# A third state's dt*u*B by TensorE in the even sequences from the fifth on, in a kernel of a selective scan and a mixture of experts

## The chip, the cores and the metric

The kernel runs on one core of one Trainium2 chip. The metric is the time of one execution on the device, in microseconds (us). One execution was profiled by the hardware; all durations, waits and windows come from it.

The core's engines work side by side, each through its own queue of instructions: PE multiplies matrices (TensorE; its weight loads are shown as PEld), DVE is VectorE, ACT is ScalarE, POOL is GpSimd, and SP is SyncE, which issues most of the DMAs.

## The reference, cut to what matters

The input is 16 sequences of 512 positions with 256 features. The first layer is a selective scan in both directions, the second a soft mixture of 16 experts; after each the input is added and normalized. The part that the change concerns is the scan. For each of 512 channels d and 16 states n:

```
dA = einsum('bld,dn->bldn', dt, A)
dB_u = einsum('bld,bld,bln->bldn', dt, u, B)
dA_cum = exp(the sum of dA over the later positions)
xs = cumsum(dB_u * dA_cum, 1) / (dA_cum + 1e-12)
y = einsum('bldn,bln->bld', xs, C) + u * D
```

So for each state, dt*u (a value for each channel and position) is multiplied by B of that state (one value for each position, the same for all channels). Then a recurrence runs along the positions, its result is gated (from the 1e-12) and multiplied by C, and all states are summed.

## The kernel before

**The scan.** A sequence b has four parts, `scan_part(b, r, p, ...)`: direction r (0 forward, 1 backward) and half p of the channels. A part has two chunks of 128 channels and runs over the 16 states in pairs (n and n + 1), so it has 8 x 2 = 16 steps; a sequence has 64 steps and the kernel 1024. A step has positions along the free axis (512) and channels on the 128 partitions. It does:

1. POOL: `db` = dt*u times B of both states, L442, B having been spread over the partitions by a DMA (`bs`, L431).
2. ACT: the decay exp(dt*A) of each state, L459, and a tanh, L461, for the gate.
3. DVE: the recurrence of each state (L465 forward, L467 backward) and the gate (L470), into `hg`.
4. POOL: `hg` times C of both states, L471 (`cs`, L432).
5. PE: transposes of `hg`, summed in PSUM over all states and both directions, L386. This is emitted two steps later (`add_up(2)`, L485), and `hg` has four buffers.

**States by TensorE.** For the states that `diag_of(b)` names (L280), step 1 is done by PE: L420 multiplies the transposed dt*u (`duT`) by a matrix that has B of the state on its diagonal (`dg`), four matmuls of 128 positions each. The result lies in a PSUM bank, and DVE's recurrence reads it there. These states are always the second of a pair. POOL's L442 is then half as wide (k = 1), the `bs` load half as large, and the decay of that state goes to SBUF (`dec`) instead of a PSUM bank of the ring `h` (three banks).

The diagonals are made in DRAM: `project_unit` writes B of the chosen states at the diagonal places of zeroed blocks with one DMA from ACT's queue (L306), once for each sequence and direction. A `dg` load (L435, 256 KB, one buffer) is issued by SP one pair of states ahead (`n + 3 in ds`). Sequences 0 to 2 have four such states (3, 7, 11, 15), all later ones two (5, 13).

**Work beside the scan.** Everything else is written as generators in three lists, `prep` (the next part's projections), `front` (the end of the sequence before: output projection, normalization, dispatch to the experts' slots) and `back` (experts and their combination, for two sequences at a time). After each scan step `beside_scan` (L556) takes at most one piece of each. A piece takes one or two PSUM banks of a pool of three (`mps`, by `bank`, L107) and holds them until the next step consumes them (`yield HOLD`). `piece` (L519) takes a piece only where the oldest bank still held, and all taken since, leave room in the three. A product of L420 takes its bank from the same pool: `by_diagonal` (L414) is called in the step before the one that uses it (L478), and L483 ends its claim.

`front` and `back` are paced: each step adds to a credit the share of the steps left (at most 2.0 is kept), and a piece costs 1. `back` gets experts(g) and combine(2g), combine(2g+1) at each odd sequence from the fourth on, spread over the 128 steps of that sequence and the following even one. So an odd sequence from the sixth on holds mostly expert work and an even one mostly combination: in each chunk of 128 positions logits `cl` (L933), their exponential, transposes `ctp` (L954), and the product `cpo` (L1015). What `front` has not done at a sequence's end is emitted at once (`front.drain()`); what `back` has not done stays in its list. After the last scan, whatever is left runs with eight banks.

The emission fixes the program order. `late(...)` marks instructions that are kept in it.

Of the kernel before, what the change touches and what calls it, by code (L numbers as in the profile page):

```python
# [55 lines left out]
def seq_layers(tc, ident, neghalf, a, out):  # L56
# [22 lines left out]
    with ExitStack() as ctx:  # L79
# [199 lines left out]

        def diag_of(b):  # L280

            return (3, 7, 11, 15) if b < 3 else (5, 13)

        def project_unit(b, r, out):

            w = side[r]
            q = f"{b}_{r}"
            yield GAP + 1
            px = bank(f"px_{q}")
            for c in range(ND):  # L290
                nc.tensor.matmul(
                    px[:XW, :], w["xT"][:, c, :], out["u"][:, c, :], start=(c == 0), stop=(c == ND - 1)
                )
            yield HOLD
            xd = p1.tile([XW, L], F32, tag=f"xd_{r}", name=f"xd_{q}")
            bc = dram.tile([2, NS, L], F32, tag="bc", name=f"bc_{q}")
            if r == 0:
                late(nc.scalar.activation(xd, px[:XW, :], AF.Identity, bias=unit))
            else:

                late(nc.scalar.activation(xd[: XB + NS, :], px[: XB + NS, :], AF.Identity, bias=unit[: XB + NS]))
                nc.scalar.copy(xd[XC:XW, :], px[XC:XW, ::-1])
            nc.sync.dma_start(bc[0], xd[XB : XB + NS, :])
            nc.sync.dma_start(bc[1], xd[XC:XW, :])
            ds = diag_of(b)
            nc.scalar.dma_start(  # L306
                diag_dram[r, : len(ds)].rearrange("i l (p s) -> i l p s", p=P)[:, :, :, 0],
                xd[XB + ds[0] : XB + NS : ds[1] - ds[0], :].rearrange("i (l p) -> i l p", p=P),
            )
            out.update(xd=xd, bc=bc)  # L310
# [96 lines left out]
        def scan_part(b, r, p, v, accs, done, then):  # L407

            prep.drain()
            prep.gens += [[1, g] for g in [turn_pair(b, r, p, v)] + then]  # L410
            w, ds = side[r], diag_of(b)
            made = {}

# [733 lines left out]
```

## Time and profile before

| | us |
|---|---|
| median of 3 runs | 5327.67 (5324.82 to 5328.87) |
| the profiled execution | 5322.25 |
| its span, first to last instruction | 5320.5 |
| busy: POOL | 4681.6 (88%) |
| busy: DVE | 4560.6 (86%) |
| busy: PE (matmul) | 4310.4 (81%) |
| busy: ACT | 4104.9 (77%) |
| sequences 4, 6, 8, 10, 12, 14 | 307.9 to 308.7 each |
| sequences 5, 7, 9, 11, 13 | 326.2 to 327.1 each |
| after the last scan | 240.4 |

A sequence is counted from the first L471 of its first step to the first L471 of the next sequence. A line of the profile gives the line of the kernel, engine, operation, what is written and read, the shapes and the count; behind the bar are the busy time and the mean duration in ns; then the idle time of the engine before them and what ended most of it. "Granted clock" is the share of PE's full clock that the throttle let through. A busy PE is not a PE at its peak, since matmuls are pipelined.

### The profile page before, as it was taken

How to read it: one execution, taken by the hardware profiler on the slowest of the kernel's cores; microseconds unless marked ns; L12 is line 12 of the kernel's file. 1: busy time of each engine (PE TensorE's matmuls, PEld its weight loads, DVE VectorE, ACT ScalarE, POOL GpSimd, SP SyncE). 2: the span in 40 equal slices, each digit the busy share in tenths (PEclk: the TensorE clock that was granted, in tenths of full speed). 3: DMA queues.
4: the chain of work that ended last, by engine and by line, in shares of the span. 5: the costliest groups of instructions: out<-in, count | busy, mean ns of one | idle time of the engine just before them, and what ended most of it. 6: DMA issues, size and time to landing. Idle time of an engine off the chain costs nothing. (4 is left out here: it accounts for less than half of the span.)

```text
span 5320.5 us, 74550 instructions
## 1 busy us (share of the span) xinstructions
PE 4310.4 (81%) x24498; PEld 3411.1 (64%) x24498; DVE 4560.6 (86%) x6284; ACT 4104.9 (77%) x6573; POOL 4681.6 (88%) x2537
## 2 busy tenths in 40 slices
PE   5677776897778978788788878889787897878889
PEld 3556565676567756676666766667666676657667
DVE  7999999889998899888898888988898889987733
ACT  6777878887888877888887887888778887777644
POOL 6999999989999899999999989998999989988710
PEclk7778888998899989999899988899888998889999
DMA  5444444675446644576446754467544664447545
GB/s 141 137 129 152 126 142 131 211 234 152 146 146 224 222 144 143 171 226 206 132 140 198 236 169 151 134 210 230 157 151 144 217 227 149 144 153 230 168 135 168
DMA packets 614820, 907.82 MB, mean 171 GB/s; under 512 B 84606, under 2 KB 404734, under 8 KB 614432
## 3 DMA queue, kind: packets, MB, share of 16 engines
q1 hardware_dynamic: 532740, 859.35, 50.9%
q10 hardware_dynamic: 81692, 43.70, 3.1%
q8 instruction: 195, 3.19, 0.2%
q14 instruction: 193, 1.58, 0.1%
HBM read 840.34 MB, written 62.56 MB: 170 GB/s over the span
## 5 line engine op out<-in xcount | busy, mean ns | idle before, releaser
L471 POOL TENSOR_TENSOR hg<-hg,cs 128x1024 f32<-128x1024 f32 x1024 | 2416.9, 2364 | 125.0 <-DVE hg L470 108.0
L442 POOL TENSOR_TENSOR db<-du,bs 128x1024 f32<-128x1024 f32 (+1 forms) x1024 | 2087.7, 2042 | 227.8 <-DVE h L465 84.1
L470 DVE SCALAR_TENSOR_TENSOR hg<-th,h 128x512 f32<-128x512 f32 x1744 | 1156.8, 679 | 183.4 <-PE acc L386 105.9
L386 PE MATMUL acc<-ident,hg 128*128 128x128 f32 x8192 | 1163.6, 292 | 106.4 <-POOL hg L471 84.6
L386 PEld LDWEIGHTS acc<-ident,hg 128*128 128x128 f32 x8192 | 1034.4, 152 | 284.6 <-POOL hg L471 131.3
L467 DVE TENSOR_TENSOR_SCAN h<-h,db 128x512 f32<-128x512 f32 x872 | 1044.9, 1219 | 104.9 <-ACT h L459 92.6
L465 DVE TENSOR_TENSOR_SCAN h<-h,db 128x512 f32<-128x512 f32 x872 | 1044.1, 1219 | 44.5 <-ACT h L459 43.6
L461 ACT ACTIVATE th<-rr,Ah_f 128x512 f32<-128x512 f32 x1024 | 724.6, 714 | 200.9 <-DVE hg L470 198.1
L461 ACT ACTIVATE th<-rr,Ah_b 128x512 f32<-128x512 f32 x1024 | 721.3, 712 | 153.5 <-DVE hg L470 143.5
L459 ACT ACTIVATE h<-dt,A_f 128x512 f32<-128x512 f32 x872 | 591.4, 680 | 99.5 <-DVE hg L470 96.3
L459 ACT ACTIVATE h<-dt,A_b 128x512 f32<-128x512 f32 x872 | 592.3, 680 | 85.6 <-DVE hg L470 81.7
L420 PE MATMUL hd<-dg,duT 128*128 128x128 f32 x2432 | 375.7, 305 | 73.2 <-ACT duT L364 27.1
L420 PEld LDWEIGHTS hd<-dg,duT 128*128 128x128 f32 x2432 | 347.9, 220 | 84.5 <-ACT duT L364 29.5
L710 PE MATMUL pl<-x2T,seT 128*128 128x512 f32 x512 | 294.1, 704 | 78.4 <-DVE hg L470 37.4
L838 PE MATMUL peo<-Wd,ht 128*128 128x256 f32 x1024 | 258.1, 408 | 63.2 <-DVE rr L346 36.6
L869 PEld LDWEIGHTS pg<-st,Wg 128*128 128x128 f32 x2048 | 243.1, 195 | 94.1 <-issue 82.8
L811 PE MATMUL pu<-st,Wu 128*128 128x128 f32 x2048 | 255.6, 284 | 49.3 <-DMA Wu<-in_Wu_dram 27.0
L1015 PE MATMUL cpo<-ceo,ct 128*128 128x256 f32 x1024 | 256.0, 407 | 43.2 <-DVE rr L346 40.0
L811 PEld LDWEIGHTS pu<-st,Wu 128*128 128x128 f32 x2048 | 245.9, 199 | 60.6 <-DVE h L467 29.5
L838 PEld LDWEIGHTS peo<-Wd,ht 128*128 128x128 f32 x1024 | 205.5, 206 | 106.1 <-DVE rr L346 39.2
L869 PE MATMUL pg<-st,Wg 128*128 128x128 f32 x2048 | 265.0, 284 | 4.5 <-DMA st<-s_dram 3.4
L1015 PEld LDWEIGHTS cpo<-ceo,ct 128*128 128x128 f32 x1024 | 207.2, 207 | 87.2 <-DVE rr L346 42.7
(165 smaller groups left out, 6754.0 us busy)
## 6 DMA issues: line engine op xcount, KB each, us to landing
cs<-bc SPq DMA_DIRECT2D x512, 512.0 KB, 3.9
bs<-bc SPq DMA_DIRECT2D x360, 512.0 KB, 5.2
Wg<-in_Wg_dram SPq DMA_DIRECT2D x128, 512.0 KB, 5.7
Wu<-in_Wu_dram SPq DMA_DIRECT2D x128, 512.0 KB, 5.8
Wd<-in_Wd_dram SPq DMA_DIRECT2D x128, 512.0 KB, 5.5
dg<-diag_dram SPq DMA_DIRECT2D x152, 256.0 KB, 4.3
bs<-bc SPq DMA_DIRECT2D x152, 256.0 KB, 3.5
x<-in_x_dram SPq DMA_DIRECT2D x32, 512.0 KB, 6.5
```

What stands on the lines that cost most here:

```text
L386: ins = nc.tensor.matmul(accs[c][:, s], hc[:, j, s], ident, is_transpose=True, start=False, stop=(last and j == 1 and lc == NL - 1),)
L420: ins = nc.tensor.matmul(h[:, s], v[c][3][:, s], dg[:, s], start=True, stop=True)
L442: nc.gpsimd.tensor_tensor(db[:, :k, :], du.unsqueeze(1).to_broadcast([P, k, L]), bs[:, :k, :], ALU.mult)
L459: nc.scalar.activation(hs[j][1], dt, AF.Exp, scale=w["A"][:, c, s])
L461: nc.scalar.activation(ths[j], rr, AF.Tanh, bias=LN_1E12 / 2, scale=w["Ah"][:, c, s])
L465: nc.vector.tensor_tensor_scan(h, dec, add, 0.0, ALU.mult, ALU.add)
L467: nc.vector.tensor_tensor_scan(h[:, ::-1], dec[:, ::-1], add[:, ::-1], 0.0, ALU.mult, ALU.add)
L470: nc.vector.scalar_tensor_tensor(hg[:, j, :], th, 1.0, h, ALU.add, ALU.mult)
L471: nc.gpsimd.tensor_tensor(hg, hg, cs, ALU.mult)
L811: nc.tensor.matmul(pu[:, fc * P : (fc + 1) * P], got["Wu", e][:, k, fc * P : (fc + 1) * P], st[:, k, :, j * SL : (j + 1) * SL], start=(k = ...
L838: nc.tensor.matmul(po[:, j * DM : (j + 1) * DM], ht[:, fc, :], got["Wd", e0 + j][:, fc, :], start=(fc == 0), stop=(fc == NF - 1),)
L869: nc.tensor.matmul(pg[:, fc * P : (fc + 1) * P], got["Wg", e][:, k, fc * P : (fc + 1) * P], st[:, k, :, j * SL : (j + 1) * SL], start=(not ...
```

## The change

One line of `diag_of`:

```
         def diag_of(b):

-            return (3, 7, 11, 15) if b < 3 else (5, 13)
+            return (3, 7, 11, 15) if b < 3 else (5, 13) if b % 2 else (5, 9, 13)
```

Sequences 4, 6, 8, 10, 12 and 14 (counted from 0) now have three states by TensorE: 5, 9 and 13. State 9 is the second of the pair n = 8. In each of the 24 parts of these sequences the two steps of n = 8 have a half-wide L442 and a half-sized `bs` load, there is one `dg` load more (at n = 6) and 8 matmuls of L420 more, and two more steps in which a product holds a bank. `project_unit` writes three rows of diagonals instead of two. Sequence 3 and the later odd ones, and 0 to 2, are as before.

## The prediction

> **What bounds the kernel now.** I read the page first, for the busy shares.
>
> ```profile
> PE 4310.4 (81%) x24498; PEld 3411.1 (64%) x24498; DVE 4560.6 (86%) x6284; ACT 4104.9 (77%) x6573; POOL 4681.6 (88%) x2537
> ```
>
> No engine is full over the span, so the stages must be told apart. A scan step ends in one product of L471 on POOL, and there are 64 steps in a sequence; the start of every 64th gives the borders of the sequences. In the windows view at these borders the columns are the stretch, its length, then busy us of PE, PEld, DVE, ACT and POOL, then the granted clock, the DMA share and GB/s. The rows are sequences 1, 3, 8 (even, touched), 9 (odd, untouched), 15, and what follows the last scan:
>
> ```profile
> 335.90:619.20 283.30, 206.80 (x1172) 168.49 (x1171) 261.16 (x323) 226.14 (x361) 275.68 (x153) 0.82 0.44 137
> 904.80:1226.30 321.50, 277.99 (x1714) 224.86 (x1715) 279.25 (x389) 257.43 (x389) 293.53 (x153) 0.94 0.66 210
> 2496.00:2804.50 308.50, 245.97 (x1282) 186.43 (x1281) 282.68 (x384) 248.87 (x417) 294.99 (x157) 0.88 0.44 140
> 2804.50:3131.50 327.00, 283.58 (x1740) 230.66 (x1738) 284.16 (x398) 261.53 (x398) 295.30 (x157) 0.94 0.67 214
> 4709.70:5080.10 370.40, 311.64 (x1830) 249.92 (x1828) 282.97 (x414) 264.99 (x416) 285.72 (x151) 0.92 0.59 186
> 5080.10:5320.50 240.40, 216.77 (x1216) 177.29 (x1214) 71.71 (x199) 97.36 (x210) 14.68 (x44) 0.97 0.52 160
> ```
>
> The reader is to see that in sequence 8 POOL has 13.5 us of idle time in 308.5 (96% busy) and PE has 62.5. In sequence 9 POOL does the same 295 us, but the sequence is 18.5 us longer, while PE has 37.6 us more work. After the last scan PE is busy for 90% of the time. Sequences 4, 6, 10, 12 and 14 lie at 307.9 to 308.7 us with the rows of 8; the odd ones from 5 to 13 at 326.2 to 327.1. The waits view (total us, times, longest) of DVE in sequence 8 and then in sequence 9 names the difference:
>
> ```profile
> DVE hg L470 <- PE acc L386: 0.8, 1, 0.8
> ```
>
> ```profile
> DVE hg L470 <- PE acc L386: 12.8, 11, 2.4
> ```
>
> In the even sequence nobody waits long for PE. In the odd one DVE's gated state waits for PE to free a buffer of `hg`, and POOL then waits for DVE. So POOL sets the pace of the sequences that the change touches, and PE helps to set it in their neighbours and after the scans.
>
> **What the change removes and adds.** The rows by form (count, then busy us, mean ns):
>
> ```profile
> L442 POOL TENSOR_TENSOR db<-du,bs 128x1024 f32<-128x1024 f32 x720 | 1699.9, 2366 | 181.2 <-issue 70.2 <-DVE h L465 56.5 <-DVE h L467 42.0
> L442 POOL TENSOR_TENSOR db<-du,bs 128x512 f32<-128x512 f32 x304 | 387.9, 1277 | 46.7 <-DVE h L465 27.5 <-POOL hg L471 11.2 <-DMA bs<-bc 4.2
> L420 PE MATMUL hd<-dg,duT 128*128 128x128 f32 x2432 | 375.7, 305 | 73.2 <-ACT duT L364 27.1 <-ACT yt L645 13.6 <-DMA dg<-diag_dram 10.2
> L933 PE MATMUL cl<-seT,cx 128*128 128x512 f32 x480 | 230.2, 620 | 32.6 <-DVE res L277 12.4 <-ACT et L725 10.7 <-DVE hg L470 7.5
> L1015 PE MATMUL cpo<-ceo,ct 128*128 128x256 f32 x1024 | 256.0, 407 | 43.2 <-DVE rr L346 40.0 <-ACT ct L963 2.5 <-DMA ceo<-e_dram 0.4
> ```
>
> Six sequences (4, 6, ..., 14) have four parts each with two chunks: 48 steps of n = 8 change.
>
> Off POOL: 48 products shrink from 2366 to 1277 ns, 1.089 us each: 8.7 us a sequence, 52.3 in all. This is the most that can be won.
>
> On PE: 48 x 4 matmuls of 305 ns = 58.6 us, 9.8 a sequence, against 62.5 of idle time: nothing. Without that cover, by the slope of odd against even (18.5 us for 37.6 of PE, 0.49), it would be 4.8 a sequence.
>
> ACT writes 48 decays to SBUF instead of PSUM (712 against 680 ns): 1.6 us in all, beside 60 us of idle time a sequence: nothing. DVE's scan (1217 against 1219 ns) and its gating (679 both) do not change. A step of n = 8 takes one `h` bank instead of two, which can only help.
>
> DMA: 24 `bs` loads halve and 24 `dg` loads of the same 256 KB come in; bytes stay. SyncE issues 24 more, 0.385 us each, and each waits for the one `dg` buffer, which is free once state 5's second chunk is multiplied, two steps earlier; `bs` and `cs` of n = 8 queue behind it, and have three buffers. In the trace 152 such loads cost PE 10.2 us of waiting in 10 places, so I expect 1 to 2 us of PE waiting: nothing. ACT's write of the diagonals takes three rows for two, two states' time before its first use: nothing.
>
> **What the 8.7 us become.** Part 1 of sequence 8 has POOL at 75.6 of 76.7 us, so there the whole 2.18 us of a part can be won; in part 0 POOL (72.6 of 78.0) is already level with DVE (72.8), so little. DVE does 282.7 us in the sequence; the smallest idle time of DVE in a sequence with other work beside the scan is 22.1 (sequence 1). DVE plus this gives 304.8, a gain of 3.7; the full POOL gain is 8.7. I take 6.5, a little over the middle, because work of DVE leaves these sequences too (next point): **39 us won**, between 22 and 52.
>
> **What the change moves.** This is no instruction of its own. A product of L420 sits in one of three `mps` banks from the step before its use, and while one sits there, `piece` (line 525) lets other work take a bank only if the oldest holder and all after it fit in three. I counted pieces by that rule on paper. In sequence 4 as it is, the three steps around each of states 5 and 13 take 3 or 4 banks of other work, and the steps around state 9 take 6 or 7, because they are free. Closing these too pushes out about 13 banks a sequence; most find room in other steps, because a piece that is refused keeps its credit up to 2. Following the queues through the four parts, I end with one more piece of dispatch to be drained at the end of sequence 4 (`pd` beside `pq`), and with 5 pieces of combine left to the next sequence instead of 1. In the later even sequences about 1 to 3 more would be left, since a longer queue comes in from the odd one. My count can be off by two or three pieces either way.
>
> The prices. A chunk of combine costs PE 8 x 0.48 + 1.25 + 4.0 = 9.1 us (L933: 230.2/60 chunks; L954: 80.0/64; L1015: 256.0/64) in three pieces: 3 us a piece.
> - Drain: 6 ends. Part 0 of the odd sequence is 2.3 us longer than its part 1 now, with one piece drained. 0 to 2.3, I take 1: 6 us.
> - Odd sequences 5 to 13: 1.7 to 3 more pieces each, some 7.5 us of PE. It may fit PE's 43 us of idle time (0) or cost by the slope above (0.49). I take half of it: 1.9 each, 9 us, between 0 and 22.
> - Sequence 15 already runs pieces at every step that lets them, so what it inherits comes out after the scans, where PE is 90% busy: 4 pieces net, 12 us of PE, I take 10, between 0 and 21.
>
> The sum: 39 won, 25 paid: 14 less than the profiled execution's 5322.25 us (span 5320.5 and 1.75 around it), 5308. The median of the runs is 5.4 above that execution, so **5314 us**, 0.26% less.
>
> A rule weighed. By matmul rows PE is 80% busy in even sequences and 87% in odd ones; by weight loads 60% and 71%. The Trainium skill, "Perfetto Trace Analysis", section "Identifying the Most-Contended Engine", says that matmul busy time is a bad measure of PE's headroom and that weight loads' busy share is a good one. By it PE is no limit in the odd sequences, the moved pieces cost nothing there, and the sum would be 9 us lower. The wait of 12.8 us on PE in sequence 9 speaks against that, so the rows keep their price.
>
> **The rivals.**
> - *All of it arrives.* The refused pieces find room within the even sequences, DVE doesn't bind: 40 to 50 us won, little paid, about 5285. For it: POOL is the only full engine there, and sequences 0 to 2 have four diagonal states with POOL at 97 to 99%. Against: these have no expert or combine work beside them. Chance 0.10.
> - *It cancels.* DVE takes POOL's place at once (22 to 25 us won), and the moved pieces eat that: about 5327. For it: POOL and DVE would be within 4 us of each other in the even sequences. Chance 0.22.
> - *Slower.* PE in the odd sequences and after the scans pays for the work pushed out: 3 pieces at 0.49 are 4.4 us in five sequences (22), 7 pieces at the end 21, drains of two pieces 12, together 55 against 30 won: 25 more, about 5350. It decides from some 5 or 6 pieces carried out of each even sequence. For it: 5 is what I count, and sequence 5 is already 4.9 us longer than 3 with 5.9 us more of PE. Against: part of that stretch is PE's idle time. Chance 0.34.
> - That the edit is not in effect: both callers of `diag_of` pass the same b, so I give it nothing.
>
> **How the numbers follow.** My forecast (5314, from 5300 to 5321) has 0.34, the largest with *slower*; I keep it since POOL's gain is priced from rows and the losses rest on a count. A difference under 0.2% (10.7 us) can't be told from no change. Faster by more has 0.34 + 0.10 = 0.44, within 0.22, slower by more 0.34. The range for 8 in 10 takes the full arrival at its low end and the slower case up to its centre: 5285 to 5350.
>
> **What would show it.** The narrow form of L442 should stand at 352, and L420 at 2624. Even sequences should last 301 to 303 us with POOL under 96%; over 306 says that DVE or PE took over. Odd ones should last about 329; at 331 and more the slower rival holds, at 327 the first one. After the last scan 250 us are expected for 240.4. Combine's products (L1015) should be found moving from even into odd sequences; if they stay, my count is wrong.

## The result, and the profile after

The changed kernel takes **5453.93 us** (median of 4 runs, 5441.44 to 5455.07) against 5327.72 for the kernel before: a ratio of **1.0232, 95% interval 1.0215 to 1.025**. It is 126 us slower. I had forecast 5314, with a range up to 5350: the sign and the range were both wrong. The profiled execution's span is 5453.0 us, 132.5 more than before's.

The page's busy shares, in the columns of the line shown first for the kernel before:

```profile
PE 4379.0 (80%) x24882; PEld 3455.5 (63%) x24882; DVE 4557.8 (84%) x6284; ACT 4102.4 (75%) x6572; POOL 4635.0 (85%) x2537
```

POOL does 46.6 us less and PE 68.6 more, as the edit says, and every share falls. So the time is not work: every engine has more idle time. The windows view of the kernel after (stretch, length, busy us of PE, PEld, DVE, ACT, POOL, granted clock, DMA share, GB/s), for the same sequences as before (1, 3, 8, 9, 15, then what follows the last scan):

```profile
335.20:619.70 284.50, 205.26 (x1181) 166.77 (x1180) 262.05 (x324) 227.12 (x363) 276.17 (x154) 0.85 0.44 137
906.00:1228.50 322.50, 279.03 (x1715) 226.20 (x1716) 279.73 (x389) 258.13 (x389) 293.65 (x153) 0.94 0.66 209
2538.70:2859.10 320.40, 251.41 (x1360) 191.32 (x1360) 279.07 (x380) 247.45 (x407) 286.85 (x157) 0.91 0.46 142
2859.10:3190.60 331.50, 281.81 (x1720) 226.99 (x1720) 287.18 (x402) 263.17 (x410) 295.74 (x158) 0.95 0.63 204
4827.30:5204.00 376.70, 313.52 (x1823) 251.64 (x1824) 280.83 (x408) 253.27 (x404) 284.17 (x147) 0.92 0.55 178
5204.00:5453.00 249.00, 230.52 (x1283) 186.80 (x1281) 77.15 (x217) 104.93 (x226) 16.45 (x49) 0.97 0.53 164
```

Sequences 1 and 3 are as they were, within 1.2 us. Sequence 8 (third row) is 12 us longer than the 308.50 of before, although POOL does 8 us less in it and DVE 3.6. Its granted clock is higher, so the clock is not the reason. Sequence 9 has 4.5 us more, 15 has 6.3, the end 8.7. Over the whole execution, from the same borders: the six even sequences +82.1, the five odd ones +33.3, sequence 15 +6.3, the end +8.7, and the start up to sequence 4 +2.2. Sequence 4, the first one touched, has already 11.5 of this (320.0 us for 308.5).

The rows by form of the kernel after, for the two instructions that the edit trades:

```profile
L442 POOL TENSOR_TENSOR db<-du,bs 128x512 f32<-128x512 f32 x352 | 453.7, 1292 | 93.6 <-DVE h L465 46.3 <-DVE h L467 39.4 <-POOL hg L471 3.9
L420 PE MATMUL hd<-dg,duT 128*128 128x128 f32 x2816 | 443.2, 308 | 214.7 <-issue 57.5 <-ACT duT L364 28.1 <-DVE rr L346 27.8
```

The edit is in effect: 48 narrow L442 more. And PE is now idle for 214.7 us ahead of its products, 73.2 before. Next the waits of sequence 8 (total us, times, longest), one fence for each of four engines: DVE, ACT, POOL and PE.

```profile
DVE h L465 <- ACT h L459: 8.6, 3, 6.1
DVE res L277 <- ACT res L274: 5.9, 2, 5.5
DVE hg L470 <- PE acc L386: 5.1, 2, 4.6
```

```profile
ACT x L625 <- POOL m_sh L620: 6.5, 1, 6.5
ACT cx L625 <- POOL rr L345: 6.1, 1, 6.1
```

```profile
POOL hg L471 <- DVE hg L470: 12.8, 7, 4.7
POOL db L442 <- DVE h L467: 7.4, 4, 2.3
```

```profile
PE hd L420 <- DVE rr L346: 7.6, 2, 4.7
PE pd L731 <- ACT et L727: 7.2, 3, 4.6
...
PE px L291 <- ACT cm L947: 4.4, 1, 4.4
```

In sequence 8 of the kernel before the first of these POOL waits was:

```profile
POOL hg L471 <- DVE hg L470: 1.6, 2, 1.1
```

The first of the DVE waits was 0.9 us there, and no single one of these DVE and POOL waits was longer than 1.1. Now there are a few long ones on DVE and POOL too. (PE had single waits of up to 6.4 us before as well.) One of them can be followed in the timeline of the kernel after (start us, us, engine, instruction, and in brackets the idle time before it with its releaser):

```profile
2813.15 5.36 PE L291 MATMUL px<-xf,xpT_f 128*80 128x512 f32 x8 [4.41 <-ACT cm L947]
...
2818.34 3.62 PE L746 MATMUL pq<-dis,xn 128*128 128x256 f32 x16
...
2821.80 1.04 PE L386 MATMUL acc<-ident,hg 128*128 128x128 f32 x8
...
2822.87 0.69 DVE L470 SCALAR_TENSOR_TENSOR hg<-th,h 128x512 f32<-128x512 f32 x1 [4.64 <-PE acc L386]
...
2825.86 4.68 POOL L471 TENSOR_TENSOR hg<-hg,cs 128x1024 f32<-128x1024 f32 x2 [4.67 <-DVE hg L470]
```

PE waits 4.41 us until ACT has read combine's logits out of a bank, then does a projection and a dispatch product back to back (9 us). Only then come the transposes that free a buffer of `hg`; DVE has waited 4.64 us for it, and POOL 4.67 us for DVE. Over the sequence PE has time enough (251 us of 320); here two pieces of other work stood in one step, and the scan waited behind them.

### The profile page after: what moved, and what is told of

It reads as the page before. It is cut to its first block, busy times and chain, and to the rows that moved or that the text cites. A ratio compares the mean times of both kernels' runs of the same rounds, so it can differ in the third digit from the quotient of the medians.

```text
span 5453.0 us, 75204 instructions
## 1 busy us (share of the span) xinstructions
PE 4379.0 (80%) x24882; PEld 3455.5 (63%) x24882; DVE 4557.8 (84%) x6284; ACT 4102.4 (75%) x6572; POOL 4635.0 (85%) x2537
## 5 line engine op out<-in xcount | busy, mean ns | idle before, releaser
L471 POOL TENSOR_TENSOR hg<-hg,cs 128x1024 f32<-128x1024 f32 x1024 | 2427.6, 2375 | 272.8 <-DVE hg L470 156.4
L442 POOL TENSOR_TENSOR db<-du,bs 128x1024 f32<-128x1024 f32 (+1 forms) x1024 | 2046.3, 2002 | 254.9 <-issue 110.4
L470 DVE SCALAR_TENSOR_TENSOR hg<-th,h 128x512 f32<-128x512 f32 x1696 | 1121.2, 677 | 214.9 <-PE acc L386 136.4
L386 PE MATMUL acc<-ident,hg 128*128 128x128 f32 x8192 | 1136.8, 287 | 111.7 <-POOL hg L471 88.3
L386 PEld LDWEIGHTS acc<-ident,hg 128*128 128x128 f32 x8192 | 1007.8, 150 | 283.4 <-issue 113.9
L465 DVE TENSOR_TENSOR_SCAN h<-h,db 128x512 f32<-128x512 f32 x848 | 1014.2, 1217 | 105.1 <-ACT h L459 98.0
L467 DVE TENSOR_TENSOR_SCAN h<-h,db 128x512 f32<-128x512 f32 x848 | 1014.9, 1218 | 91.9 <-ACT h L459 74.7
L459 ACT ACTIVATE h<-dt,A_b 128x512 f32<-128x512 f32 x848 | 575.7, 680 | 79.6 <-DVE hg L470 76.7
L420 PE MATMUL hd<-dg,duT 128*128 128x128 f32 x2816 | 443.2, 308 | 214.7 <-issue 57.5
L420 PEld LDWEIGHTS hd<-dg,duT 128*128 128x128 f32 x2816 | 402.2, 220 | 235.5 <-issue 81.0
L1015 PE MATMUL cpo<-ceo,ct 128*128 128x256 f32 x1024 | 258.2, 411 | 61.1 <-DVE rr L346 25.3
L710 PE MATMUL pl<-x2T,seT 128*128 128x512 f32 x512 | 263.6, 639 | 33.2 <-DVE rr L346 23.2
L933 PE MATMUL cl<-seT,cx 128*128 128x512 f32 x480 | 245.6, 651 | 43.4 <-ACT sl L756 18.3
L1015 PEld LDWEIGHTS cpo<-ceo,ct 128*128 128x128 f32 x1024 | 209.6, 209 | 103.9 <-issue 28.6
```

The lines of the kernel that those rows point to most:

```text
L386: ins = nc.tensor.matmul(accs[c][:, s], hc[:, j, s], ident, is_transpose=True, start=False, stop=(last and j == 1 and lc == NL - 1),)
L420: ins = nc.tensor.matmul(h[:, s], v[c][3][:, s], dg[:, s], start=True, stop=True)
L442: nc.gpsimd.tensor_tensor(db[:, :k, :], du.unsqueeze(1).to_broadcast([P, k, L]), bs[:, :k, :], ALU.mult)
L459: nc.scalar.activation(hs[j][1], dt, AF.Exp, scale=w["A"][:, c, s])
L465: nc.vector.tensor_tensor_scan(h, dec, add, 0.0, ALU.mult, ALU.add)
L467: nc.vector.tensor_tensor_scan(h[:, ::-1], dec[:, ::-1], add[:, ::-1], 0.0, ALU.mult, ALU.add)
```

## The experiments

Every run is timed against the kernel before on the same chip (its median there lay between 5327 and 5332). e2, e4, e6, e7, e10, e11, e15 and e18 were executed twice, up to 17 us apart; the intervals say what that allows. "Even", "odd", "15" and "end" are the differences of the profiled execution from before's in the six even sequences, the five odd ones, sequence 15 and after the last scan; they come from one execution each, and in e17, whose time is that of before, they differ by up to 3 us. One product slot of a state has three parts in the program, and the experiments take them apart: the **product** itself (L420); its **claim** on the bank pool (`diags.append`, which leaves others' pieces less room in three steps around it); and the **early taking-up** (L478: work that holds banks is consumed before the product is emitted).

### What POOL's time is worth

**e1_pool_alone.** POOL's saving without anything else of the change, on the kernel before (state 9 then takes state 8's B):

```
+            extra = {9} if b >= 4 and b % 2 == 0 else set()
...
+                m = 1 if n + 1 in extra else k
...
-                nc.sync.dma_start(bs[:, :k, :], v["bc"][0, n : n + k, :].unsqueeze(0).to_broadcast([P, k, L]))
+                nc.sync.dma_start(bs[:, :m, :], v["bc"][0, n : n + m, :].unsqueeze(0).to_broadcast([P, m, L]))
...
-                        db[:, :k, :], du.unsqueeze(1).to_broadcast([P, k, L]), bs[:, :k, :], ALU.mult
+                        db[:, :m, :], du.unsqueeze(1).to_broadcast([P, m, L]), bs[:, :m, :], ALU.mult
...
-                            hs[j] = (h, dec, db[:, j, :])
+                            hs[j] = (h, dec, db[:, min(j, m - 1), :])
```

> The kernel before, with the narrow product on GpSimd (and the half-sized load of B) at the steps of n = 8 in the six even sequences, and nothing on TensorE for it: state 9 uses state 8's B, so that one input of the computation is another one. If GpSimd bounds these sequences, as I forecast, 6.5 us come off each of them: about 5289 us, between 5276 and 5306. If VectorE takes over at once: 5306 to 5316. If GpSimd isn't the bound at all: 5325 to 5330.

Measured: 5326.31 against 5331.88, ratio 0.9989 (0.9979 to 0.9998). The windows row of its sequence 8:

```profile
2496.40:2804.20 307.80, 243.29 (x1278) 184.34 (x1278) 282.34 (x384) 248.44 (x417) 286.81 (x157) 0.88 0.44 137
```

POOL is down by 8.2 us and the sequence by 0.7. The 39 us that I had counted as won are 6 (by the interval 1 to 11). POOL's freed time became idle time.

**e8_no_max** (the three row maxima of combine's softmax left out in the even sequences, its exponential taking a quarter of the logits instead) and **e9_no_max_pool** (this and e1's edit together) ask whether DVE then binds:

```
-            late(nc.vector.reduce_max(nm[:, 0:1], cls[0], AX.X))
...
+            by, scale = (none, 0.25) if touched[0] else (nm[:, 2:3], 1.0)
+            if not touched[0]:
+                late(nc.vector.reduce_max(nm[:, 0:1], cls[0], AX.X))
```

> The kernel before, with the maxima of the combining softmax left out in the six even sequences (the exponential takes a quarter of the logits and no shift, so combination weights are others there): 1.5 us of VectorE less for each of 8 chunks, 12 us a sequence, 72 in all, and one hop less between cl and its exponential. If VectorE is what bounds these sequences: 5265 to 5285 us. If it isn't: 5315 to 5330.

> The run without the maxima and the run with GpSimd's narrow product at n = 8 put together (both leave out what those left out). The narrow product alone gave 6 us. If VectorE hides GpSimd's gain, it gives 25 to 45 us here on top of the run without maxima; if GpSimd's time is slack for another reason (the order of its queue), again 0 to 10.

Measured: e8 5325.55, ratio 0.9995 (0.9983 to 1.0006), even +9.7, odd -7.6; e9 5312.36, ratio 0.9964 (0.995 to 0.9978). So of 107 us taken from POOL and DVE together (52 and 55 by their busy times), 18 came off the time. In e9, sequence 10 and, because it was named before, 8:

```profile
3127.40:3435.80 308.40, 245.70 (x1286) 186.18 (x1286) 274.01 (x361) 248.03 (x418) 286.51 (x158) 0.89 0.44 137
2496.20:2800.80 304.60, 241.31 (x1286) 181.14 (x1286) 274.11 (x361) 248.13 (x418) 286.53 (x158) 0.90 0.44 138
```

Sequence 10 stands for the rest: 308.4 us, 307.9 in the kernel before, with POOL 22 us under the length, DVE 34 and PE 63. Sequence 8 is the only even one that gained more than 1 us (3.9), and the six together gained the same 3.9 in this execution. So neither POOL nor DVE is *the* bound, nor both. I take it that a chain through all of them binds. I followed the releasers back from the last L471 of sequence 8 of the kernel before, by the rule of the chain view: of 306 us DVE has 139, ACT 54, PE 46, waiting for nothing shown ("issue") 48, and POOL 19. An engine that is 96% busy holds 6% of this chain, and DVE 45%.

### Which part of a product slot costs

**e3_h_ring.** The change, with state 9's product in the `h` ring: no claim, no early taking-up (`extra` is as in e1, here and below).

```
+                if n in extra:
+                    made[n, c] = h = ps_h.tile([P, L], F32, tag="h", name=f"hd_{b}_{r}_{n}_{c}")
+                else:
+                    diags.append(count[0])
+                    made[n, c] = h = bank(f"hd_{b}_{r}_{n}_{c}")
...
-                        for x in sides:
+                        for x in sides if nxt_n + 1 not in extra else ():
...
-                    if k == 1:
+                    if k == 1 and n + 1 not in extra:
                         diags.pop(0)
```

**e2_claim_only.** The kernel before, with claim and early taking-up at state 9 and no product:

```
                         by_diagonal(nxt_n + 1, chunks[1] if c == chunks[0] else chunks[0])
+                    elif nxt_n + 1 in extra:
+                        for x in sides:
+                            x.take_up()
+                        diags.append(count[0])
+                        count[0] += 1
                     beside_scan()
-                    if k == 1:
+                    if k == 1 or n + 1 in extra:
                         diags.pop(0)
```

**e7_claim_h_ring.** The change with claim, early taking-up and product, but the product in the `h` ring (e3's first part, with `diags.append(count[0])` kept and `count[0] += 1` beside it).

> The changed kernel, but state 9's product goes into a bank of the ring that holds h (which a step of n = 8 uses once instead of twice), and makes no claim on the three banks, so the other work stands where it stood before. If the claim makes the loss: 5285 to 5310 us, the gain of the narrow product alone. If the product's matmuls, its diagonal load or the decay in SBUF make it: 5400 us or more.

> The kernel before, with only the claim on one of the three banks at the steps around state 9 (the early take-up, an entry in the list of claims, the count raised by one), no product, no diagonal load and no narrow product. The changed kernel lost 126 us, and about 39 more if GpSimd's gain is real. If the claim makes the loss by moving the other work: 5440 to 5490 us, the even sequences at 325 us or more. If the product itself makes it (its matmuls stand in TensorE's queue until a bank is free): 5330 to 5360.

> The changed kernel with the claim, the early take-up and all products as they are, but state 9's product lies in the ring of h and no longer in one of the three banks (the count still rises by one). The claim alone cost 86 us, the whole change 126 while its narrow product should give 6. If the 45 us left are the bank itself, which the other work lacks: 5405 to 5420 us. If they are the product's matmuls in the changed order: 5440 to 5460.

| | us | ratio (95%) | even | odd | 15 | end |
|---|---|---|---|---|---|---|
| the change | 5453.93 | 1.0232 (1.0215 to 1.025) | +82.1 | +33.3 | +6.3 | +8.7 |
| e3: no claim | 5322.68 | 0.9986 (0.9976 to 0.9995) | -8.6 | +6.5 | +1.3 | +1.0 |
| e2: claim, no product | 5418.22 | 1.0161 (1.0141 to 1.0182) | +62.3 | +18.6 | +1.6 | +10.3 |
| e7: claim, product in the ring | 5420.60 | 1.017 (1.014 to 1.0199) | +66.9 | +16.2 | +2.9 | +10.1 |

e3 has all of the change's work, and costs nothing. Its sequence 8 stands at 306.9 us, with POOL at 286.7:

```profile
2495.20:2802.10 306.90, 247.41 (x1336) 188.03 (x1336) 280.22 (x382) 248.06 (x416) 286.66 (x157) 0.90 0.46 141
```

e2 has none of the work, and costs 86 us of the 126 (5418.22 less 5331.88). The change's work on top of the claim, with POOL's saving in it, makes 2 us (e7 less e2), which is within the two intervals. So the 126 us come from the product's place in the bank pool and from nothing else in the change. e2's windows for sequences 4, 6 and 8 and the end show where the claim is paid:

```profile
1227.60:1536.80 309.20, 230.42 (x1204) 172.74 (x1203) 277.09 (x372) 243.67 (x402) 295.25 (x158) 0.88 0.45 139
1868.70:2187.70 319.00, 249.36 (x1296) 189.26 (x1296) 279.17 (x381) 247.12 (x405) 295.57 (x158) 0.87 0.47 142
2517.60:2839.60 322.00, 248.11 (x1296) 188.36 (x1296) 279.37 (x381) 247.15 (x406) 295.58 (x158) 0.88 0.44 141
5163.90:5414.50 250.60, 232.20 (x1287) 188.25 (x1285) 77.20 (x217) 105.41 (x227) 16.46 (x49) 0.96 0.53 163
```

Sequence 4 has the same closed steps as 6 and 8, and is 0.7 us longer than before. It hands work on: PE does 230 us in it, 246 in the kernel before. From 6 on nearly the same PE work as before (249 and 248 in 6 and 8, before 243 and 246) takes 10 to 14 us more. The records in the windows show what moved, in e2 as in the change: each even sequence has 96 of L1015 (before 112) and each odd one from 5 to 13 has 32 (before 16); and of the experts' last product (`peo`) each even sequence from 6 on has 16 records, one expert of eight, where it had none. Sequence 4 gives work away and takes none in. So I read it that with the claim alone most of the price is not paid where pieces are refused, but where the refused pieces come in.

The rest of the change, 33 us (5453.93 less e7's 5420.60), comes when the product really sits in one of the three banks. Of the even sequences it lengthens mainly sequence 4 (320.0, e7 307.9; all six together 15 us), and the five odd ones by 17 together. I take it that pieces wait there for the bank itself; no run isolates that.

**e10_claim_no_take_up** is e2 without its two `take_up` lines; **e11_take_up_only** is e2 with only these; **e4_one_take_up** is the change with `beside_scan(nxt_n + 1 not in extra)`, which leaves out the second taking-up of a step.

> The claim alone once more (no product, GpSimd as before), but without the early take-up: the two steps only enter a claim and raise the count. The claim with the take-up cost 86 us. If shutting the other work out of the steps around state 9 makes that cost: 5390 to 5425 us. If the second take-up in a step makes it: 5330 to 5355.

> The counterpart: the kernel before with only the early take-up at the two steps before state 9's use, no claim, no product. If shutting out makes the cost of the claim: 5320 to 5345 us. If the second take-up does: 5390 to 5420.

> The changed kernel with one take-up instead of two at the steps in which state 9's product is issued, so that other work's consumers are not advanced by two stages in one step. If the second take-up makes the loss (ScalarE's scaling comes too close behind GpSimd's factors, 66 us more of ScalarE's idle time in the even sequences): 5330 to 5390 us. If the places of the work matter and not this: 5435 to 5460.

Measured: e10 5432.43, ratio 1.0188 (1.0168 to 1.0208), even +65.9, odd +24.0, end +10.2. e11 5371.36, 1.0073 (1.0053 to 1.0094), even +35.6, odd +3.7, 15 +7.4, end -0.1. e4 5434.76, 1.0192 (1.017 to 1.0214). So the claim alone gives the whole of e2. The early taking-up alone costs 40, and without handing anything on: e11's even sequences are all 314.2 to 314.4 with the work of before. Beside a claim it costs nothing more. The second taking-up is worth about 19 us (5453.93 less 5434.76), and e4's two executions lie 17 us apart. The two prices don't add.

**e6_after_consts.** ACT's longest waits in the change are for POOL's normalization factors (the two fence lines of ACT above). The change with constants in their place in the even sequences:

```
         def scaled(dst, src, sh, rs):
+            if touched[0]:
+                sh, rs = none, ones
```

> The changed kernel, but in the six even sequences ScalarE's scalings of x and cx (two layer norms) take a constant 0 and 1 instead of GpSimd's factors: the normalization is left out there, GpSimd still computes the factors, ScalarE no longer waits for them. In the changed kernel ScalarE sits idle 66 us more than before in front of these scalings. If that wait makes the loss in the even sequences: 5385 to 5400 us. If the wait only stands in the place of another: 5435 to 5460.

Measured: 5435.85 against 5330.38, ratio 1.0198 (1.0169 to 1.0228). Some 18 of the 126 us go, though 66 us of ACT's waits in the even sequences of the change carry that label. So most of these waits stand in the place of others.

### Is it any shift of the work, or late work?

**e17_credit** starts the credits of `front` and `back` at 0.5 in the even sequences, **e19_no_gaps** lets their pieces ignore the gaps there, **e18_front_first** always lets `front` go ahead of `back` there; all on the kernel before, without a claim:

```
+            if b >= 4 and b % 2 == 0:
+                front.credit = back.credit = 0.5
```

```
-            hurry = b + 1 == nb
+            hurry = b + 1 == nb or (b >= 4 and b % 2 == 0)
```

```
-            for x in (front, back) if front.credit > back.credit else (back, front):
+            for x in (front, back) if front.credit > back.credit or touched[0] else (back, front):
```

> The kernel before, with half a credit given to front and back at the start of each even sequence from the fifth on: the same work in the same sequences (what is left at each end is the same, by a count of the pieces), only some pieces stand one or two steps earlier. If the loss of the claim comes from work that is carried out of the sequence or finds less room: 5322 to 5340 us. If any shift of the other work against the scan costs, because the order before is a good one among many worse: 5345 to 5430.

> The kernel before, with front ahead of back in every step of those even sequences. By a count of the pieces back then leaves 11 units to the next odd sequence and 20 at the end of the scans (1 and 9 before; the changed kernel 5 and 17). If the carried work is what costs: more than the claim's 86 us, 5420 to 5480. If the places within the even sequences cost, and carried work little: 5335 to 5400.

> The kernel before, without the pause that a piece makes after its own list was taken up (gaps) in those even sequences: the same work in the same sequences, denser chains. If any shift costs: 5350 to 5430 us. If only lost room costs: 5315 to 5340.

Measured: e17 5324.50, ratio 0.999 (0.9979 to 1.0001). e19 5326.14, 0.9993 (0.9981 to 1.0004), even +23.6 and odd -20.4. e18 5468.48, **1.0263 (1.0222 to 1.0304)**, even +111.6, odd +17.2, end +29.3. The windows of e18 for sequence 10 and the end:

```profile
3177.10:3515.30 338.20, 262.74 (x1422) 204.12 (x1423) 284.29 (x386) 255.31 (x411) 294.96 (x158) 0.88 0.50 153
5205.60:5475.30 269.70, 245.26 (x1312) 196.75 (x1311) 80.87 (x225) 105.98 (x231) 16.34 (x49) 0.95 0.50 152
```

In e17 and e19 pieces are moved about within the pair of sequences, and that costs nothing (what the even ones lose in e19 the odd ones win); e11 has shown that it can. Holding `back` back costs as much as the whole change (139 us; two executions, 17 us apart), without a claim or a product: by its program order 11 of `back`'s units are left at the end of an even sequence, 1 in the kernel before, 5 in the change. So late work can make a loss of this size. That it is the handing on which costs is not shown by this run: sequence 4, which takes in nothing, is already 11.0 us longer in it, 6 and 8, which take in one and two experts of eight (by the records of `peo`), 11.7 and 10.1, and only 10 to 14, with three, 23 to 30.

### Do claims cost in themselves?

If so, taking away the claims of states 5 and 13 would win. **e12_before_ring** puts all products from sequence 3 on into the `h` ring, without claims and early taking-up (e3's diff with `b >= 3` for `n in extra`); **e13_after_ring** is the same on the change.

> The kernel before (states 5 and 13), but from sequence 3 on their products lie in the ring of h and make no claim on the three banks, with no early take-up. If claims are what is dear, the claims of 5 and 13 cost too and this is well below the kernel before: 5150 to 5290 us. If only a third claim in a part is dear, because two leave room enough: 5310 to 5335.

> The changed kernel's states (5, 9, 13 in the even sequences) with all products from sequence 3 on in the ring of h and no claims. Against the run with 5 and 13 in the ring: 5 to 10 us less if GpSimd's time stays off the path in the even sequences as it did, 25 to 45 less if the freer order of the other work puts it on the path. Slower than that run only if the ring of three banks gets too tight with a third product.

Measured: e12 5558.46, ratio 1.0425 (1.0408 to 1.0443), even +98.5, odd +115.7, sequences 0 to 3 +26.9 (3 is the only one of these that the edit touches), end -10.0; e13 5544.79, 1.0399 (1.0383 to 1.0414). **That theory finds no support.** Work beside the scan finishes sooner (the end is 10 us shorter), and yet every touched sequence is longer; in the odd ones the idle time of DVE put down to `hd` of PE goes from 17.6 to 113 us. Whether the ring of three is too short for a product more, or pieces that are free to come early stand in PE's queue ahead of the products, these runs don't tell apart. Against the first stands that a third product in the ring costs nothing more: e13 is 14 us under e12.

**e14_before_five_h**, **e15_after_five_h** and **e16_h_ring_five_h** were to lengthen that ring, on the kernel before, on the change and on e3: the first state's decay of a full step goes to two SBUF buffers.

```
                         if j < k:
-                            dec = h = ps_h.tile([P, L], F32, tag="h", name=f"h_{q}_{c}_{j}")
+                            if j == 0 and k == 2:
+                                dec = h = p4.tile([P, L], F32, tag="dec", name=f"h_{q}_{c}_{j}", bufs=2)
+                            else:
+                                dec = h = ps_h.tile([P, L], F32, tag="h", name=f"h_{q}_{c}_{j}")
```

> The kernel before, with the first state's h of each full step in one of the two SBUF buffers of dec instead of the PSUM ring, so that five buffers serve what three served, and ScalarE's decays can run further ahead of VectorE. If the handover between ScalarE and VectorE through three banks paces the even sequences, where neither GpSimd's nor VectorE's work did: 5200 to 5300 us. If the work's order alone sets the time: 5310 to 5340. If two operands in SBUF slow VectorE's scan beside GpSimd, its row says so and the time is above 5400.

> The changed kernel with the same five buffers. If the tight ring is why a moved piece of other work costs so much (ScalarE stops for it and VectorE runs dry after three decays), this stands less than 60 us above the kernel before with five buffers, where it stood 126 above it with three. If the ring isn't why: 110 to 140 us above.

> The run with state 9's product in the ring of h and no claim, plus the five buffers: the best of both if the buffers help. 5 to 10 us under the kernel before with five buffers if GpSimd stays off the path, 30 or more under it if the buffers let its gain through.

Measured: 6499.79, 6492.46 and 6360.93 (ratios 1.2191, 1.2178 and 1.193; intervals within 0.003 of each). As a test of the ring they fail, for a reason of their own (last section). e15 is 7 us below e14, which by the words of its expectation would make the tight ring the reason; but e16 is 139 us below e14, so in this slower kernel the third state by TensorE wins by itself, and e14 is no base for e15. What compares is e15 less e16, the change's bank against the ring: 131.5 us, and without the five buffers (the change less e3) 131.3. So nothing here says that a deeper ring makes the claim cheaper. That the two agree so closely is chance in part: in the even sequences it is 119 us with the five buffers and 91 without.

No kernel beats the one before clearly with the whole computation. The nearest is e3, 0.9986 (0.9976 to 0.9995): the same third state by TensorE, in a bank that asks nobody for room.

## Why the prediction was wrong, point by point

- **POOL's saving: wrong, 39 won against 6.** The failed step is "So POOL sets the pace of the sequences". I read a 96% share as a pace. e1 took 48.9 us from POOL (52.3 expected), e9 also 8.0 us from DVE in sequence 10 (282.0 to 274.0), and the sequences hardly moved. The waits view had hinted at it: of POOL's 13.5 us of idle time in sequence 8, 6.3 are put down to "issue" and 4.0 to DVE. My "nobody waits long for PE" had left out DVE's 4.0 us for `pl` and 5.3 us for the products there. I had tested the gain by busy sums (DVE plus 22.1), and a sum of busy time bounds a chain only from below.
- **The product on PE costs nothing: right** (e3, and e7 less e2 within the noise). My 58.6 us for it came out of a wrong count: a product is 8 records, not 4 matmuls of 305 ns, so L420 stands at 2816 and not at the 2624 that I gave as a sign. Records overlap: 375.7 us for 304 products is 1.24 each, 59.3 for 48. Measured: 67.5.
- **ACT, DVE and the `dg` loads at nothing: right** (all in e3).
- **The count of displaced work at the end of an even sequence: right.** In the program order after the change `pd` and `pq` are both drained there, only `pq` before, and 5 units of `back` are left against 1. What I did not price is that the odd sequence then hands an expert on to the next even one.
- **Its price in the even sequences: wrong, and this is the step that failed most.** "Most find room in other steps" gave a price of zero. The claim alone made these sequences 62 us longer (e2), 66 (e10), the whole change 82. Why is in part argued: the timeline above shows one case of two pieces in a step with the scan waiting behind them, and the windows of e2 show the loss where an expert comes in from the odd sequence. I priced the work handed on by PE's time, a sum again; in the waits of the change DVE and POOL stand idle behind it.
- **The odd sequences: 9 for 33**, above my 0 to 22 (with the claim alone 19 in e2 and 24 in e10). **The end: 10 for 9.** There PE is busy for nine tenths of the time, and pricing by PE's time came out; sequence 15 has 6 more that I had at nothing.
- **A bank in fact taken: not in the sum, 33 us.** I priced the room in the count of banks and gave the bank itself no price. What its cost consists of is not shown.
- **The rivals.** *Slower* was the one, with its mechanism of handed-on work (5 units, its point of decision). Its size, 25, left the even sequences out, and it still set 30 won against it. Of my signs, the odd sequences at 331 us and more and the 249 us at the end spoke for it; but "over 306 says that DVE or PE took over" was wrong: the even ones last 320 to 326 us, and no engine took over.

The terms together: 86 for the claim, 2 for the work with POOL's saving in it, and 33 for the bank make 122 against the base of e2; the change's own base is 4 us lower, hence 126. They are steps from one kernel to the next and so add up whatever they are; as e10 and e11 show, the same steps taken singly need not. What stays open is which handover makes the 62 us: in e2 DVE's idle time for `h` of ACT doubles in the even sequences (43 to 98 us), but no run changes it alone. Why e11 and e12 cost, with nothing handed on, is not settled either; they say that the order within a sequence matters as well as how much is late.

A rule of the skill and these runs. By the windows of the even sequences POOL has the highest share, 96%, and taking 3% of its work away there gained 0.1% of the time. The Trainium skill, "Perfetto Trace Analysis", section "Identifying the Most-Contended Engine", takes the engine with the highest occupancy as the most contended and would optimize it first. For this kernel the measurement decides against that: e1 followed the rule and gained 6 us for 49 taken from POOL.

## What to carry to other kernels

An engine that is 96% busy need not be the bound: take its saving out alone, before counting on it. In a program whose order is written out by hand, price a new claim on a shared bank by who is refused, when he comes instead and who waits behind him; it cost 86 us here, with no instruction added, and the work itself was free in a ring that the work beside the scan does not use. A price of zero for displaced work ("it finds room") needs a run of its own: hold the place, do nothing in it, and measure.

## What the runs showed of the hardware

e14 to e16 cost 19 to 22%; e14 has no more instructions on DVE, POOL or PE than the kernel before. What changed is the place of one tile, from PSUM to SBUF: the first state's decay in each full step, in which DVE's recurrence also leaves its result and which the gate then reads. By form, DVE's gate and its backward recurrence, then POOL's product, in e14:

```profile
L473 DVE SCALAR_TENSOR_TENSOR hg<-th,h 128x512 f32<-128x512 f32 x1744 | 1783.7, 1042 | 134.1 <-PE acc L386 56.5 <-ACT th L464 36.0 <-POOL hg L474 2.2
L470 DVE TENSOR_TENSOR_SCAN h<-h,db 128x512 f32<-128x512 f32 x872 | 1404.2, 1628 | 72.9 <-ACT h L462 71.1 <-issue 1.7
```

```profile
L474 POOL TENSOR_TENSOR hg<-hg,cs 128x1024 f32<-128x1024 f32 x1024 | 2827.1, 2764 | 260.3 <-DVE hg L473 183.0 <-issue 17.7 <-PE peo L841 16.6
```

And the same three in the kernel before:

```profile
L470 DVE SCALAR_TENSOR_TENSOR hg<-th,h 128x512 f32<-128x512 f32 x1744 | 1156.8, 679 | 183.4 <-PE acc L386 105.9 <-ACT th L461 39.4 <-ACT et L725 0.8
L467 DVE TENSOR_TENSOR_SCAN h<-h,db 128x512 f32<-128x512 f32 x872 | 1044.9, 1219 | 104.9 <-ACT h L459 92.6 <-POOL db L442 11.5
L471 POOL TENSOR_TENSOR hg<-hg,cs 128x1024 f32<-128x1024 f32 x1024 | 2416.9, 2364 | 125.0 <-DVE hg L470 108.0 <-PE cpo L1015 5.7 <-issue 4.3
```

The means grew by 53, 34 and 17%, and DVE became 90% busy. The row of the gate mixes 720 products whose operand was moved with 1024 whose operand was not: its median is 678 ns, as before (677), and its longest is 2836 (691). ACT's busy time grew by 0.3% (4117.8 us against 4104.9). The Trainium skill, "SBUF — State Buffer", section "Who interferes with whom", says that a DVE instruction with two SBUF inputs contends with a GpSimd instruction that reads SBUF, through a port pair that one of them locks. These rows agree, and give it a size for this kernel; which of the moved tile's three uses costs how much, no run tells apart.
